# Moving the layer norm's affine by two slots in a two-layer scan kernel, with the counts that a planner reads

## The chip, the cores and the metric

The kernel runs on one core of a Trainium2 chip. The time is the device time of one execution in microseconds (us); the median of several executions is compared. A profiled execution shows what each engine did: PE (TensorE, matrix products), DVE (VectorE), ACT (ScalarE), POOL (GpSimd), and SP, whose queue issues nearly all transfers.

## What is computed

The input has 2 batches of 256 channels by 4096 positions, all in float32. Layer 0 is a state-space block (a "mamba" block); layer 1 normalises its result, runs a forward and a backward state-space block over it, and ends with a mixture of eight experts, all of which are computed for every position. Cut to what matters:

```python
# layer 0
x = x + mamba(group_norm(x))                     # inner width 256
# layer 1
t = tokens(x)
n = layer_norm(t)
xn = layer_norm(n) * ln_gamma + ln_beta          # the second norm ends with the affine
t = t + mamba_fwd(xn) + flip(mamba_bwd(flip(xn))) + n    # inner width 512
# experts, over the norm of t
f = layer_norm(t)
w = softmax(mean_over_batch(f) @ Wr + br)
t = t + sum_e w[e] * (relu(bn2(relu(bn1(f @ W1[e])) @ W2[e])) @ Wo[e] + bo[e])

def mamba(x):
    xs, z = split(x @ W_in)
    xs = silu(causal_conv4(xs))
    dt, B, C = ...                               # projections of xs, dt through softplus
    h[t] = exp(dt[t] * A) * h[t-1] + dt[t] * xs[t] * B[t]    # 16 states for each channel
    y = sum_over_states(h * C) + xs * D
    return (y * silu(z)) @ W_out
```

## The kernel before

**Tiling and order.** There are six scan jobs: for each batch, layer 0 (2 tiles of 128 inner channels), the forward block of layer 1 (4 tiles) and the backward block (4 tiles). Each job runs over 8 chunks of 512 positions. A chunk of layer 0 has 16 slots and a chunk of layer 1 has 32, so there are 1280 slots in all. Two slots make a quad: four groups of 512 positions by 128 partitions, of which each partition is one channel and state. In each slot DVE runs one scan instruction (L690) of 1024 elements, and all other work is hung on slots. `s0` is the first slot of a chunk; a slot before `s0` belongs to the chunk that runs before it.

**What a quad needs.** POOL multiplies `dt*x` by B into `bq` (L654, one operation for the quad). ACT makes the decays: it corrects the first element of a half with the carried state (the join, L675) and then takes two exponentials into a PSUM tile `da` (L664), of which there are two buffers (pool `ps_d`); it does so one slot ahead of the scan. DVE scans. The product with C is taken by DVE (L699) or, for quads 0, 2 and 5 of each 8 and some halves, by POOL (L714 copies the state out, L715 multiplies). PE then sums over the states (L723). ACT copies the state out for the halves that DVE multiplied (the carry, L709).

**What sets the order.** Each engine's instructions run in the order in which the loop over slots emits them. Within a slot the order is: SP's own work, loads that have become due, PE, PE's expert products, ACT, DVE, POOL. On ACT the carry and the decays of the next slot stand first, and what was put on the slot's "act" list follows. So late work on ACT delays the decays of the slot after the next.

**Work around the affine.** For layer 1's forward job, `norm` prepares the next chunk: `mean`, `centre`, `square`, `variance`, `roots`, `divide`, `add`, `affine` and `store` are put on slots counted from that chunk's `s0`. `affine` (L387) is two ACT operations that write `nx`, the input of the projections; `add` (L383) on POOL reads `nx` before that; `store` writes `nx` and the sum `x` to DRAM (L393, L394). In the same slots the chunk that is running ends: ACT loads the table of functions for the gate (L569) at slot 26 of its 32, the four gates' tanh (L539) run in slots 27, 28, 30 and 31, and at slot 29 ACT makes the values for the next chunk's joins (the cut, L616 and L619).

**Expert pairs.** A pair is one batch, one chunk and one expert, with three layers of two products each; each product is one entry in the plan (called an expert layer in what follows, so six to a pair), 4 PE instructions, and one ACT operation (L923, or L921 for the third layer). The pairs of the chunks whose norm is ready (`features`, in the backward jobs) are placed beside the scans by the planner in `experts`. It knows what each slot has of PE and ACT work from `sl.count(slot, products, acts, banks)`, which books PE's products on the slot and ACT's operations on the next one, and keeps two backlogs:

```python
PE_ROOM, PE_BEHIND = 3.8, 2.5
ACT_ROOM, ACT_BEHIND = 2.6, 1.2
...
                behind = max(0.0, behind) + sl.products.get(slot, 0) + sums_in(slot) - PE_ROOM
                act_behind = max(0.0, act_behind) + sl.acts.get(slot + 1, 0) - ACT_ROOM
...
                    if behind + 2 > PE_BEHIND or act_behind + 1.3 > ACT_BEHIND or not fits(slot):
                        break
```

`fits` asks whether one of three PSUM banks of the pool `psp` is free. Their results go to DRAM (`u`).

**The tail.** What is left is done after the scans: for each chunk of `rest` the pairs that are missing (L1208 for two layers, L1227 for the third), with the router's weights (`routes`: `n` loads, `nm` on POOL at L1115, logits on PE at L1122) and the sums with the results from DRAM (`sums`, L1178 and L1179) beside them. `whole` has the chunks of which all 16 pairs are done. `rest` is sorted by how many pairs of a chunk are done, and otherwise keeps the order from chunk 7 down to 0:

```python
        rest.sort(key=lambda i: sum(first[b, i] for b in range(NB)))
```

Of the kernel before, what the change touches and what calls it, by code (L numbers as in the profile page):

```python
# [131 lines left out]
def hybrid_kernel(ctx: ExitStack, tc: tile.TileContext, a: dict, out: bass.AP):  # L132
# [45 lines left out]
    def rsqrt(dst, src, eps, scale=1.0):  # L178
        nc.scalar.activation(dst, src, AF.Ln, bias=eps, scale=scale)
        nc.scalar.activation(dst, dst, AF.Exp, scale=-0.5)  # L180

    def over_channels(t):
        return t.rearrange("p (o t) -> p o t", o=1).to_broadcast([P, KC, T])


    with ExitStack() as st:
# [30 lines left out]
        sl = Slots()  # L217
# [98 lines left out]
        def norm(i):  # L316

            (job, c), ck, tag, s0 = steps[i], cks[i], tags[i], starts[i]
            s = job.cols(c)
            b = job.batch  # L320

            def alloc():
                ck["nx"] = wk.tile([P, KC, T], F32, tag="nx", name=f"nx_{tag}", bufs=2)

            if job.flip:
                def load():
                    alloc()
                    nc.sync.dma_start(ck["nx"], n2_dram[b][:, NCH - 1 - c, :, :])
                sl.put(s0 - 44, "sp", load)
                return  # L330

            def load_x():
                ck["x"] = wk.tile([P, KC, T], F32, tag="x", name=f"x_{tag}")
                src = t_dram[b] if job.layer else a["x"][b].rearrange("(k p) l -> p k l", p=P)
                nc.sync.dma_start(ck["x"], src[:, :, s])

            if job.layer == 0:
                def scale():
                    alloc()
                    for k in range(KC):  # L340
                        nc.scalar.activation(
                            ck["nx"][:, k, :], ck["x"][:, k, :], AF.Identity,
                            bias=job.gb[:, k : k + 1], scale=job.gs[:, k : k + 1],
                        )
                sl.put(s0 - 32, "sp", load_x)
                sl.put(s0 - 25, "act", scale)
                return

            def mean():
                ck["ps"] = psp.tile([P, T], F32, tag="ps", name=f"mean_{tag}")
                for k in range(KC):
                    nc.tensor.matmul(
                        ck["ps"], mean_w, ck["x"][:, k, :], start=(k == 0), stop=(k == KC - 1)
                    )

            def centre():
                ck["cen"] = wk.tile([P, KC, T], F32, tag="cen", name=f"cen_{tag}")
                nc.vector.tensor_tensor(ck["cen"], ck["x"], over_channels(ck["ps"]), ALU.subtract)  # L360

            def square():
                alloc()
                nc.scalar.activation(ck["nx"], ck["cen"], AF.Square)

            def variance():
                ck["var"] = psp.tile([P, T], F32, tag="ps", name=f"var_{tag}")
                for k in range(KC):
                    nc.tensor.matmul(
                        ck["var"], mean_w, ck["nx"][:, k, :], start=(k == 0), stop=(k == KC - 1)  # L370
                    )

            def roots():
                ck["r1"] = psp.tile([P, T], F32, tag="ps", name=f"r1_{tag}")
                rsqrt(ck["r1"], ck["var"], eps5)
                rsqrt(ck["var"], ck["var"], eps10, scale=1.0 + 1e-5)

            def divide():
                nc.vector.tensor_tensor(ck["nx"], ck["cen"], over_channels(ck["r1"]), ALU.mult)
                nc.vector.tensor_tensor(ck["cen"], ck["cen"], over_channels(ck["var"]), ALU.mult)  # L380

            def add():
                nc.gpsimd.tensor_tensor(ck["x"], ck["x"], ck["nx"], ALU.add)  # L383

            def affine():
                for k in range(KC):
                    nc.scalar.activation(  # L387
                        ck["nx"][:, k, :], ck["cen"][:, k, :], AF.Identity,
                        bias=lngb[:, 1, k : k + 1], scale=lngb[:, 0, k : k + 1],
                    )  # L390

            def store():
                nc.sync.dma_start(n2_dram[b][:, c, :, :], ck["nx"])  # L393
                nc.sync.dma_start(t_dram[b][:, :, s], ck["x"])  # L394

            for d, queue, fn in (
                (-48, "sp", load_x), (-44, "pe", mean), (-43, "dve", centre), (-42, "act", square),
                (-41, "pe", variance), (-40, "act", roots), (-39, "dve", divide), (-39, "pool", add),
                (-37 if c else -38, "act", affine), (-36, "sp", store),
            ):  # L400

                sl.put(s0 + d + (6 if c == 0 else 0), queue, fn)
            s0 += 6 if c == 0 else 0
            sl.count(s0 - 44, 2, 0, (1,))
            sl.count(s0 - 43, 0, 1)
            sl.count(s0 - 41, 2, 4, (2,))
            sl.count(s0 - 40, 0, 0, (1,))
            sl.count(s0 - 38, 0, 2)

        def in_proj(job, ck, half, j, name):  # L410
            ps = psp.tile([P, T], F32, tag="ps", name=name)
# [564 lines left out]
        for i in range(len(steps)):  # L976
            norm(i)
            prepare(i)
            load_later(i)
            finish(i)  # L980
# [420 lines left out]
```

## Time and profile before

| | us |
|---|---|
| runs, median of 3 (lowest, highest) | 5132.12 (5131.54, 5132.48) |
| the profiled execution | 5134.52 |
| its span, first to last instruction | 5132.7 |
| first scan of the second forward job (the fifth job) | at 2749.3 |
| first scan of the last backward job | at 3628.3 |
| end of the last scan | 4504.8 |
| first L1208 of the tail | 4543.7 |

| group of the profile | count | mean |
|---|---|---|
| POOL L654, `bq` from `rxdt` and B | 640 | 4543 ns |
| DVE L690, scan | 1280 | 2278 to 2350 ns (medians of its four forms) |
| ACT L664, one decay exponential | 2560 | 686 ns |
| ACT L387, half of an affine | 32 | 802 ns (median) |
| ACT L569, load of a function table | 96 | 1283 ns |
| PE L912, expert product beside the scans | 1920 | 613 to 620 ns |

Each engine is counted busy from the start to the end of its instructions. A wait is put down to what ended it. Below, "a stretch" is a span of time in us from the first instruction, and for each engine its busy time in the stretch and the number of its instructions are given.

### The profile page before, as it was taken

To read this page: it belongs to the slowest core of one execution; us is meant where nothing else is said; L and a number is where in the kernel's file an instruction comes from. 1 tells how busy PE (TensorE), PEld (TensorE's weight loads), DVE (VectorE), ACT (ScalarE), POOL (GpSimd) and SP (SyncE) were. 2 spreads that over 40 slices of the span, in tenths; PEclk is the share of its full clock that TensorE was granted. 3 is DMA by queue.
4 is the path that set the end of the run, shared out by engine and by line. 5 is a ranking of instruction groups with operands and counts; after the bars stand their busy time and mean duration, and the time that the engine had idled before them with its cause. 6 is when DMAs were issued, how large, how long until landed. Compare 5 with 4: busy or idle time off the path is not lost.

```text
span 5132.7 us, 47350 instructions
## 1 busy us (share of the span) xinstructions
PE 4283.0 (83%) x14920; PEld 1485.7 (29%) x14920; DVE 4581.7 (89%) x3088; ACT 3681.3 (72%) x7474; POOL 4410.3 (86%) x1442
## 2 busy tenths in 40 slices
PE   5677767776668988888988888899999999888999
PEld 1222222221122323333322233233333333333444
DVE  6998999999999999999989999999999999936543
ACT  5777677777767888888888788888778878832232
POOL 5998999999999999999989999999999999911100
PEclk8888888887888999999999999999999999999999
DMA  5454433344444454546654555455554444455532
GB/s 178 149 176 158 164 136 128 132 146 144 151 139 156 170 195 163 184 165 209 207 185 170 174 181 179 159 167 177 195 187 166 167 165 161 168 180 182 191 108 77
DMA packets 321355, 845.49 MB, mean 165 GB/s; under 512 B 35720, under 2 KB 107152, under 8 KB 279120
## 3 DMA queue, kind: packets, MB, share of 16 engines
q1 hardware_dynamic: 316816, 815.07, 46.2%
q0 software_dynamic: 4288, 27.40, 1.4%
q8 instruction: 118, 1.93, 0.2%
q14 instruction: 133, 1.09, 0.1%
HBM read 655.05 MB, written 187.30 MB: 164 GB/s over the span
## 4 chain that ended last, share of the span: by engine, by line
DVE 20%; PE 15%; ACT 10%; issue 4%; POOL 3%; DMA 2%; SPq 0%; DVEq 0%; POOLq 0%; ACTq 0%
DVE da L690 9%; PE hp L1208 5%; DVE bq L699 5%; ACT da L664 4%; PE y L1227 2%; PE e L912 2%; DVE bq L690 2%; POOL bq L654 2%; PE conv L452 1%; POOL bq L715 1%; PE y L723 1%; ACT bq L675 1%; DVE x L1179 1%; DVE u L1178 1%; ACT eh L923 1%
## 5 line engine op out<-in xcount | busy, mean ns | idle before, releaser
L654 POOL TENSOR_TENSOR bq<-rxdt,bc 128x2048 f32<-128x2048 f32 x640 | 2893.2, 4543 | 28.7 <-issue 12.3
L664 ACT ACTIVATE da<-rdt,w_a 128x512 f32<-128x512 f32 x2560 | 1756.8, 686 | 105.4 <-DVE bq L690 59.8
L690 DVE TENSOR_TENSOR_SCAN da<-da,h_state,bq 128x1024 f32<-128x1024 f32 x664 | 1559.1, 2348 | 50.5 <-ACT da L664 34.4
L715 POOL TENSOR_TENSOR bq<-bq,bc 128x2048 f32<-128x2048 f32 (+1 forms) x280 | 1179.9, 4214 | 22.5
L690 DVE TENSOR_TENSOR_SCAN bq<-da,h_state,bq 128x1024 f32<-128x1024 f32 x456 | 1059.3, 2338 | 28.5 <-ACT da L664 28.4
L723 PE MATMUL y<-bq,stack 128*32 128x512 f32 x5120 | 759.4, 687 | 317.4 <-POOL bq L715 297.3
L699 DVE TENSOR_TENSOR bq<-da,bc 128x1024 f32<-128x1024 f32 x760 | 926.5, 1219 | 16.0
L912 PE MATMUL e<-eh,ew 128*128 128x512 f32 x1280 | 626.1, 620 | 66.0 <-DVE sp L513 15.0
L709 ACT COPY h_state<-da 128x2 f32<-128x2 f32 x759 | 119.1, 157 | 641.3 <-DVE bq L699 639.4
L675 ACT ACTIVATE bq<-h_state,bq,a 128x1 f32<-128x1 f32 x1120 | 430.5, 384 | 0.6
L723 PEld LDWEIGHTS y<-bq,stack 128*32 128x32 f32 x5120 | 143.6, 119 | 876.7 <-POOL bq L715 404.9
L1212 ACT ACTIVATE h<-hp,of,sc 128x512 f32<-128x512 f32 x192 | 149.1, 777 | 298.9 <-PE hp L1208 281.7
L912 PEld LDWEIGHTS e<-eh,ew 128*128 128x128 f32 x1280 | 230.3, 193 | 452.0 <-issue 219.4
L414 PE MATMUL xs<-nx,w_in 128*128 128x512 f32 x640 | 318.7, 628 | 40.9 <-DVE xc L466 20.8
L452 PE MATMUL conv<-xs,w_conv 64*64 64x512 f32 x2560 | 332.6, 613 | 21.9 <-ACT xs L436 18.9
L414 PE MATMUL z<-nx,w_in 128*128 128x512 f32 x640 | 323.8, 639 | 18.7 <-DVE sp L513 10.6
L912 PE MATMUL e<-en,ew 128*128 128x512 f32 x640 | 308.3, 613 | 23.9 <-DVE fcen L809 7.8
L761 PE MATMUL o<-sz,w_out 128*128 128x512 f32 x640 | 301.7, 612 | 0.0
L923 ACT ACTIVATE eh<-e,of,sc 128x512 f32<-128x512 f32 x320 | 242.1, 768 | 36.7 <-PE e L912 36.2
L517 POOL TENSOR_TENSOR xdt<-sp,xc 128x512 f32<-128x512 f32 x160 | 203.2, 1273 | 49.9 <-DVE sp L513 49.8
L730 PE MATMUL y<-xc,w_d 128*128 128x512 f32 x320 | 193.1, 688 | 54.2 <-DVE sz L742 53.9
L690 DVE TENSOR_TENSOR_SCAN da<-da,bq 128x1024 f32<-128x1024 f32 x96 | 219.4, 2286 | 6.5 <-ACT da L664 3.6
(139 smaller groups left out, 4940.5 us busy)
## 6 DMA issues: line engine op xcount, KB each, us to landing
rxdt<-xdtd SPq DMA_DIRECT2D x160, 1024.0 KB, 6.8
rdt<-dtd SPq DMA_DIRECT2D x160, 1024.0 KB, 6.5
bc<-bcd SPq DMA_DIRECT2D x384, 256.0 KB, 3.2
dtd<-sp SPq DMA_DIRECT2D x160, 256.0 KB, 3.5
xdtd<-xdt SPq DMA_DIRECT2D x160, 256.0 KB, 4.0
ew<-in_W SPq DMA_DIRECT2D x160, 256.0 KB, 4.3
u<-u SPq DMA_DIRECT2D x80, 512.0 KB, 4.4
u<-eu SPq DMA_DIRECT2D x76, 512.0 KB, 4.0
```

Source lines behind the costliest of these rows:

```text
L414: nc.tensor.matmul(ps, job.w["in", half][:, k, j * P : (j + 1) * P], rhs, start=(k == 0), stop=(k == KC - 1),)
L452: nc.tensor.matmul(v[r][64 * col : 64 * col + 64, :], job.w["conv"][rows, 2 * jp + j, k, :], ck["xs", jp][rows, j, k : k + T] if k < 4 els ...
L654: nc.gpsimd.tensor_tensor(bq[g], ck["rxdt", j], over_groups(ck["bc", 0, sg]), ALU.mult)
L664: nc.scalar.activation(da[g, h][:, k, :], cks[i]["rdt", j][:, q, :], AF.Exp, scale=steps[i][0].w["a"][:, j, q * SG + sg : q * SG + sg + 1],)
L675: nc.scalar.activation(bq[g][:, q, 0:1], job.h[:, j, sg, q : q + 1], AF.Identity, scale=cks[i]["a0", j][:, h, sg : sg + 1], bias=bq[g][:, ...
L690: nc.vector.tensor_tensor_scan(b if on_pool(g, h) else d, d, b, job.h[:, j, sg, 2 * h : 2 * h + 1] if c else 0.0, ALU.mult, ALU.add,)
L699: nc.vector.tensor_tensor(bq[g][:, two, :], d, cks[i]["bc", 1, sg].rearrange("p (o t) -> p o t", o=1).to_broadcast([P, 2, T]), ALU.mult,)
L715: nc.gpsimd.tensor_tensor(b, b, cks[i]["bc", 1, sg].rearrange("p (o t) -> p o t", o=1).to_broadcast([P, groups, T]), ALU.mult,)
L723: nc.tensor.matmul(y[i, j][q * CG : (q + 1) * CG, :], stack, bq[g][:, q, :], start=False, stop=(sg == SG - 1),)
L761: nc.tensor.matmul(v[m], job.w["out"][:, j, m * P : (m + 1) * P], ck["sz", j], start=False, stop=(j == job.nj - 1),)
L912: nc.tensor.matmul(ps, ew[l][:, k, m * P : (m + 1) * P], key[x][:, k, :], start=(k == 0), stop=(k == KC - 1),)
L923: nc.scalar.activation(key[dst][:, m, :], key["ps", l, m], AF.Relu, bias=of[:, l, e, m : m + 1], scale=sc[:, l, e, m : m + 1],)
```

## The change

`affine` of chunks 1 to 7 is put two slots later (from slot `s0 - 37` to `s0 - 35`); that of chunk 0 keeps its slot. `store` of all chunks is put two slots later. What the planner is told of the affine changes: for chunks 1 to 7 it is booked on ACT two slots later, for chunk 0 one slot earlier, where it runs, and with 2.3 operations instead of 2.

```diff
@@ norm
                 (-41, "pe", variance), (-40, "act", roots), (-39, "dve", divide), (-39, "pool", add),
-                (-37 if c else -38, "act", affine), (-36, "sp", store),
+                (-35 if c else -38, "act", affine), (-34, "sp", store),
             ):
 
                 sl.put(s0 + d + (6 if c == 0 else 0), queue, fn)
...
             sl.count(s0 - 40, 0, 0, (1,))
-            sl.count(s0 - 38, 0, 2)
+            sl.count(s0 - (36 if c else 39), 0, 2.3)
```

Nothing else is edited. The planner places the pairs anew from these counts, so the slots of expert work, the number of pairs beside the scans, and `first`, `rest` and the order of chunks in the tail follow from them.

## The prediction

> **What bounds the kernel now.** I read the page first (parts 1 and 2), then busy time by stretch, then the waits of POOL and of DVE in the same stretches, then single places on the timeline. From the page:
>
> ```profile
> span 5132.7 us, 47350 instructions
> PE   5677767776668988888988888899999999888999
> DVE  6998999999999999999989999999999999936543
> ACT  5777677777767888888888788888778878832232
> POOL 5998999999999999999989999999999999911100
> ```
>
> Up to the 35th slice (4505 us) DVE and POOL are both full; then PE alone is. So there are two regimes: the scans, and a tail of 628 us with the expert pairs that were not done beside the scans. The stretches are the first forward scan of layer 1 (526.70), the second (2749.30), chunks 1 to 6 of the second backward scan (3737.50), and the tail's pairs (4543.70):
>
> ```profile
> core 0: us, PE busy (x) PEld busy (x) DVE busy (x) ACT busy (x) POOL busy (x), PEclk, DMA share, GB/s
> 526.70:1399.20 872.50, 609.89 (x2310) 182.02 (x2312) 855.16 (x557) 635.76 (x1341) 867.99 (x278) 0.82 0.40 140
> 2749.30:3628.30 879.00, 779.17 (x2851) 267.89 (x2850) 856.62 (x557) 715.89 (x1476) 870.43 (x278) 0.95 0.51 174
> 3737.50:4399.70 662.20, 596.57 (x2182) 206.05 (x2181) 641.70 (x415) 533.11 (x1115) 646.45 (x205) 0.96 0.51 173
> 4543.70:5113.40 569.70, 546.06 (x1321) 238.76 (x1322) 277.82 (x262) 168.63 (x228) 75.44 (x54) 0.97 0.43 153
> ```
>
> In the scans POOL has only 4.5, 8.6 and 15.8 us free, DVE 17.3, 22.4 and 20.5. A microsecond of DVE idle costs time only where POOL comes to wait for it. POOL's waits are listed in one row of each stretch that the change touches (the first forward scan has no such row at all); the first row is the second forward scan, the others the second backward scan without its last chunk, POOL then DVE:
>
> ```profile
> POOL h_state L714 <- DVE bq L690: 4.0, 4, 1.5
> ...
> POOL h_state L714 <- DVE bq L690: 12.4, 10, 1.5
> ...
> DVE bq L690 <- ACT da L664: 11.1, 7, 2.2
> DVE da L690 <- ACT da L664: 6.4, 9, 1.8
> ```
>
> Now the place that the change is about: the affine (L387) and the first gate (thz) of chunk 2 to 3 of the second forward scan, on ACT, then the DVE scan that came late by it, then POOL at that moment:
>
> ```profile
> 3063.66 0.58 ACT L539 ACTIVATE thz<-z 128x512 f32<-128x512 f32 x1
> 3064.14 1.51 ACT L387 ACTIVATE nx<-cen,lngb 128x512 f32<-128x512 f32 x2
> 3065.55 0.37 ACT L675 ACTIVATE bq<-h_state,bq,a 128x1 f32<-128x1 f32 x1
> ...
> 3063.81 2.36 DVE L690 TENSOR_TENSOR_SCAN da<-da,h_state,bq 128x1024 f32<-128x1024 f32 x1 [0.45 <-issue]
> ...
> 3062.87 2.35 POOL L715 TENSOR_TENSOR bq<-bq,bc 128x1024 f32<-128x1024 f32 x1
> 3065.17 4.55 POOL L654 TENSOR_TENSOR bq<-rxdt,bc 128x2048 f32<-128x2048 f32 x1
> ```
>
> DVE lost 0.45 us; POOL ran on without a gap, so this stall was paid for already. And a stall of another kind, in the second backward scan:
>
> ```profile
> 3973.66 1.42 ACT L664 ACTIVATE da<-rdt,w_a 128x512 f32<-128x512 f32 x2 [1.79 <-DVE bq L690]
> ...
> 3971.28 2.34 DVE L690 TENSOR_TENSOR_SCAN bq<-da,h_state,bq 128x1024 f32<-128x1024 f32 x1
> 3975.11 2.35 DVE L690 TENSOR_TENSOR_SCAN bq<-da,h_state,bq 128x1024 f32<-128x1024 f32 x1 [1.48 <-ACT da L664]
> ```
>
> Here the decay exponentials of a scan could start only when the scan just before it had ended: they were given the PSUM buffer of that scan instead of the other of the two. DVE stood for 1.48 us.
>
> [...] the gap of 1.48 us comes again at the same slot of chunks 0, 1, 2, 3, 5 and 6 of the backward scan. [...] In this trace they nearly agree (L654 lasts 4.55 us, and two in a row start 4.50 us apart), so I use POOL's waits as they stand.
>
> **The change part by part.**
>
> Affine two slots later (14 of 16 chunks; chunk 0 keeps its slot). It adds no instruction. It takes 1.51 us of ACT from a slot that lasts 2.26 us and puts it into one of 3.97 us. There it meets the cut (L616, L619: 0.47 + 0.30), often one expert activation (0.77) and the standing work (carry 0.17, join 0.40, decays 1.42): 5.04 us of ACT, 1.07 more than the slot. The next slot is 3.52 us with about 3.3 us of ACT work; together 8.4 against 7.5, but the decays must be in time, not the trailing expert work (1.35 us), so I charge nothing. The affine overwrites what POOL's add reads; its waits for that (3.0 us in 4 cases) can only shrink. The consumer, the input projection, is still four slots away. First forward scan: POOL never waits, gain 0. Second: at most the 4.0 us of POOL's waits.
>
> Stores two slots later. The two stores of a chunk (n2 and t) move on SP's queue past one rxdt load (chunk 0: past one weight load), in the second scan past an expert weight load too; these are now issued ahead of them. Behind the stores stand bc1 loads (3.2 us from issue to landing in part 6), first wanted some four slots (13 us) later. Cost 0; if that cover went, at most 3 us a chunk. The x buffer, read by the store, is wanted again some 18 slots later: 0.
>
> The planner's counts. This is the larger effect. Evaluating the planning loop with the new counts gives 81 pairs instead of 80 (on PE the built order has 486 rows of expert matmuls for 480). Expert layers per chunk of the second forward scan go from 16 14 16 17 15 16 21 20 to 16 16 18 18 18 18 22 19; both versions leave 8 layers after the last scan. Three consequences:
>
> 1. One pair fewer in the tail. PE is busy 546.1 of 569.7 us there, so it is the bound; a pair is 24 matmuls, and undisturbed pairs follow each other every 10.6 us (L1208 at 5063.8, 5074.4, 5085.0). Gain 10.6. The pair taken over is batch 1, chunk 5, expert 0, which moves chunk 5 from first to last of the tail; with chunk numbers renamed the rest of the sequence is the same, its largest wait (PE for POOL's nm, 12.4 us) included: 0. Its addition costs two DVE operations and one load of 512 KB, beside PE: 0.
>
> 2. The extra pair beside the scans: 14 us of PE and 4.3 us of ACT, spread over slots with ACT free for some 20 us a chunk: 0, apart from stalls in item 3.
>
> 3. Another pattern of expert work per slot. In the order of the built kernels with their waits, the decays of the sixth slot of a 16-slot group wait for DVE (the bad buffer) in 21 groups of 80 before and in 15 after; the six that go are chunk 4 of the second forward scan and chunks 1, 2, 3, 5, 6 of the second backward scan. No new one appears. Each is 1.48 us of DVE: 7.4 in the backward scan. In exchange five chunks there take the pattern that chunks 3 and 6 of the forward scan had, which shows 0.6 us of idle DVE at slots 6 and 7, but loses the 0.64 at slot 18. What comes back is bounded by POOL's 12.4 us of waits. DVE needs 107 us busy plus about 2 idle, POOL about 108, per chunk of 110.4: I take 8. Bounds: 3 (the new pattern eats most) to 12.4. In the forward scan, of POOL's 4.0: chunk 4's wait (1.0) goes with its stall, of chunk 7's 2.6 about half, since its bad buffer stays. I take 2.5, bounds 0 and 4.
>
> Last chunk of the scans: 34 layers for 36, two bad buffers stay: 0 ± 1.5. Passage to the tail (38.9 us): the same 8 layers and stores: 0 ± 1.
>
> Sum: 10.6 + 8 + 2.5 = 21.1. The profiled execution took 5134.5 us (span 5132.7 and 1.8 around it), so 5113.4; the median of the runs, 5132.1, is 2.4 lower: 5111.
>
> **The rivals.**
> A. Only the tail gains: POOL holds the pace in the backward scan as well, or the new pattern's stalls replace the old. For it: POOL's 646 of 662 us. Against: 12.4 us of waits. 5132.1 - 10.6 = 5121.5, to 5119.
> B. Every DVE stall was time: DVE, not POOL, sets the scans. For it: DVE at 97%; the affine's stalls and chunk 6's 2.1 us at slots 27 and 28 (about 4.5), six bad buffers (8.9), chunk 0's 4.0 at slots 27 and 28 of the backward scan, a forward-scan stall of 2.2: about 20, with 10.6 some 31, so 5101. Against: POOL without gaps at the affine.
> C. Slower: the denser packing makes ACT late. For it: chunk 1 of the second forward scan, where an ACT copy waited for PE and DVE then stood 2.2 us at slot 7. If each of the twelve chunks 1 to 6 of the two later scans paid that (26), and each of seven affines the 1.07 us of its overfull slot (7.5), with POOL's slack used up, it would be 34 - 7.4 for the bad buffers - 10.6 = +16: 5148. It decides from 18 us in all, 1.4 a chunk. Against: ACT is free for 20 us of such a chunk, and chunks 3 and 6, which had the dense start, lost 0.6.
> D. The change does less than it says: the 81st pair is done beside the scans but the tail gives its 10.6 back at the reordered end, by waits of PE for the last chunk's sums. About 5122, or 5130 if the scans gain nothing too.
>
> **How the numbers follow.** Forecast 0.62, A 0.17, B 0.12, C 0.05, D 0.04. The forecast's own bounds: the least of it is 10.6 + 3 + 0 - 1.5, 5120, the most 10.6 + 12.4 + 4 + 1.5, 5103.6. A's end takes the range to 5121, the nearer part of B to 5102. A measurement of this kernel can tell about 0.2% from no change, 10.3 us, that is 5121.9. The forecast, B and 0.12 of A lie below it: 0.86; D and the other 0.05 of A: 0.09; C: 0.05.
>
> **What would show it.** The tail's pairs, from first L1208 to last, about 10.6 us shorter, and the end of the last scan about 10 us earlier. POOL's waits for DVE in the second backward scan 4 to 5 us instead of 12.4; the 1.48 us stall gone in five of six chunks. The first forward scan within 1 us of 872.5 although its affine moved. I am wrong in mechanism if the first forward scan shortens by several us, or if POOL's waits fall and the stretch does not; wrong in size if the tail's wait for nm grows beyond 12.4.

## The result and the profile after

The changed kernel takes 5111.89 us (median; 5107.34 to 5113.05), the kernel before 5131.83 us in the same series. The ratio is 0.9961 (95% interval 0.9951 to 0.9971), so 20 us or 0.4% less. The prediction was 5111. The profiled execution has a span of 5111.0 us, 21.7 below the 5132.7 of before.

First the page's head and its slices of the changed kernel, in the rows of before:

```profile
span 5111.0 us, 47355 instructions
...
PE   5777767776668988988888889999999999988999
...
DVE  6998999999999999999989999999999999936633
ACT  5777677777767888888887888888878888832232
POOL 5998999999999999999989999999999999921110
```

The two regimes are as they were; nothing new is full. Where the time went shows only by stretch. The rows give start and end, length, then busy time of PE, PE's loads, DVE, ACT and POOL, the clock, the DMA share and GB/s. They are the first forward scan, the second, chunks 1 to 6 of the second backward scan, the passage from the last scan to the first L1208, and the tail's pairs:

```profile
526.30:1398.80 872.50, 607.67 (x2310) 181.47 (x2312) 855.08 (x556) 635.57 (x1341) 867.99 (x278) 0.82 0.40 139
2748.90:3625.10 876.20, 787.06 (x2890) 271.56 (x2889) 857.08 (x556) 721.17 (x1486) 869.99 (x278) 0.96 0.52 177
3732.90:4389.90 657.00, 599.93 (x2177) 202.72 (x2176) 641.91 (x415) 533.89 (x1113) 647.30 (x206) 0.97 0.52 173
4495.00:4533.70 38.70, 25.18 (x62) 10.04 (x62) 1.95 (x3) 7.40 (x11) 2.32 (x5) 0.87 0.35 121
4533.70:5092.30 558.60, 532.14 (x1297) 232.53 (x1298) 276.62 (x263) 165.60 (x225) 74.49 (x54) 0.97 0.45 158
```

Against before: 0 in the first forward scan, 2.8 less in the second, 5.2 less in the six backward chunks (chunk 0 of that scan gave 1.4 more), 0.2 in the passage, 11.2 in the tail. The last scan ended at 4495.0 instead of 4504.8. POOL's busy time in the backward row did not fall (646.45 to 647.30) while the row fell by 5.2; so it is POOL's waiting that went. DVE's busy time did not fall either (641.70 to 641.91), so its idle time fell as much. These are POOL's waits in the second forward scan and in backward chunks 1 to 6, then DVE's in the latter (total us, times, longest):

```profile
POOL h_state L714 <- DVE bq L690: 1.5, 1, 1.5
...
POOL h_state L714 <- DVE bq L690: 6.3, 6, 1.5
...
DVE sp L513 <- ACT h_state L709: 8.4, 6, 2.1
DVE da L690 <- ACT da L664: 2.3, 6, 0.7
DVE xc L466 <- ACT thx L461: 1.4, 5, 0.3
```

POOL's waits were 4.0 and 12.4. DVE's waits in the same six chunks of the kernel before:

```profile
DVE bq L690 <- ACT da L664: 7.4, 5, 1.5
DVE sp L513 <- ACT h_state L709: 5.8, 6, 1.1
DVE da L690 <- ACT da L664: 4.2, 7, 0.7
```

Its first row, which holds the five stalls of 1.48 us, is gone. In exchange the softplus on DVE (L513) waits 8.4 us for ACT where it waited 5.8. One row fell and another grew: the experiments had to take these apart.

One reading in the prediction was wrong. It showed 0.45 us of idle DVE beside the affine as the affine's stall. This is the same place of the changed kernel, ACT first and then DVE:

```profile
3058.17 1.28 ACT L569 ACT_TABLE_LOAD   x1
3059.47 0.78 ACT L923 ACTIVATE eh<-e,of,sc 128x512 f32<-128x512 f32 x1
3060.14 0.38 ACT L675 ACTIVATE bq<-h_state,bq,a 128x1 f32<-128x1 f32 x1
3060.42 1.40 ACT L664 ACTIVATE da<-rdt,w_a 128x512 f32<-128x512 f32 x2
...
3067.70 1.51 ACT L387 ACTIVATE nx<-cen,lngb 128x512 f32<-128x512 f32 x2
...
3061.91 2.36 DVE L690 TENSOR_TENSOR_SCAN da<-da,h_state,bq 128x1024 f32<-128x1024 f32 x1 [0.45 <-POOL h_state L714]
```

The affine is now 6 us away and the gap is still 0.45 us. The scan starts when its decays end (3060.42 + 1.40), and these stood behind the table load (1.28 us) and an expert activation (0.78). Before, too, the affine started only after that scan had (3064.14 against 3063.81), so it cannot have held it up; the lines shown in the prediction already said so. Neither place shows a scan that came late by the affine.

### The profile page after: what moved, and what is told of

It is laid out like the page before. It is cut to its first block, busy times and chain, and to the rows that moved or that the text cites. A ratio compares the mean times of both kernels' runs of the same rounds, so it can differ in the third digit from the quotient of the medians.

```text
span 5111.0 us, 47355 instructions
## 1 busy us (share of the span) xinstructions
PE 4272.0 (84%) x14920; PEld 1474.5 (29%) x14920; DVE 4580.6 (90%) x3089; ACT 3682.0 (72%) x7476; POOL 4409.1 (86%) x1442
## 5 line engine op out<-in xcount | busy, mean ns | idle before, releaser
L709 ACT COPY h_state<-da 128x2 f32<-128x2 f32 x759 | 118.9, 157 | 617.7 <-DVE bq L699 615.4
L452 PE MATMUL conv<-xs,w_conv 64*64 64x512 f32 x2560 | 332.1, 608 | 21.7 <-ACT xs L436 17.8
```

Source lines behind the costliest of these rows:

```text
L452: nc.tensor.matmul(v[r][64 * col : 64 * col + 64, :], job.w["conv"][rows, 2 * jp + j, k, :], ck["xs", jp][rows, j, k : k + T] if k < 4 els ...
```

## The experiments

All runs beside the kernel before on the same chip. The last table of this section has their stretches.

**1. The affine alone.** The planner's counts as before, so the old plan with 80 pairs:

```diff
-                (-37 if c else -38, "act", affine), (-36, "sp", store),
+                (-35 if c else -38, "act", affine), (-34, "sp", store),
```

> The kernel before with the affine and the stores two slots later, but with the old planner counts, so 80 pairs and the old pattern of expert work. My theory: POOL has no gap at the affine, so moving it gives nothing: 5132 us, within 2 us of before; the 32 reused PSUM buffers and POOL's 12.4 us of waits in the second backward scan stay. Rival (the affine's place matters): half or all of the gain outside the tail, 5 to 9 us, so 5123 to 5127, with the forward scans shorter.

Measured: ratio 0.9999 (0.9991 to 1.0007), median 5131.96 us. The move that gave the change its name is worth nothing that can be measured; a rival that needed 5 us or more lies outside the interval. In its profile the second forward scan was 2.1 us shorter (876.9), POOL's waits there 2.0 instead of 4.0, which the total does not resolve.

**2. The counts alone.** The affine and the stores at their old slots:

```diff
-            sl.count(s0 - 38, 0, 2)
+            sl.count(s0 - (36 if c else 39), 0, 2.3)
```

> The kernel before with only the new planner counts: affine and stores at their old slots, 81 pairs, the new pattern of expert work. My theory: nearly all of the gain, 5112 us within 2, with the backward scan shorter by some 6.6 us as in the changed kernel. Rival (the affine has to make room first): ACT is too full at the old slots, 5115 to 5121.

Measured: ratio 0.9960 (0.9948 to 0.9972), median 5112.49 us. This one line is the whole gain. Chunks 1 to 6 of the backward scan took 657.8 us, as in the changed kernel; the affine does not have to make room. The line makes three changes at once, which were not timed one by one. Worked out with the planning loop alone, the 2.3 by itself leaves the old plan as it is, and the shift of chunks 1 to 7 by two slots gives the new 81 pairs, with one expert layer one slot off; with the booking of chunk 0 moved too it is the new plan exactly.

**3. The changed kernel without the 81st pair.**

```diff
-            emit_experts(put)
+            emit_experts(put[:80])
```

> The changed kernel with everything of its plan but the 81st pair (batch 1, chunk 5, expert 0), which goes back to the tail. My theory: the tail's pairs cost 10.6 to 11.2 us each, so 5122.5 to 5123 us, with the end of the last scan where the changed kernel has it (4495, at most 1 us earlier). Rival D of the prediction (the tail gives the pair back by its order): 5112 to 5114.

Measured: ratio 0.9967 (0.9954 to 0.9980), median 5115.83 us, where I had expected 5122.5 to 5123. The median is 4 us above that of the changed kernel, but the two intervals overlap, and the profiled execution, the fastest of its executions, is no longer than the changed kernel's (span 5110.2 against 5111.0). So the pair is worth between nothing and some 4 us, and not 11. These are the passage and the tail of this kernel:

```profile
4494.20:4522.00 27.80, 14.55 (x39) 5.57 (x37) 1.90 (x2) 3.12 (x5) 1.93 (x4) 0.83 0.39 131
4522.00:5091.10 569.10, 546.53 (x1321) 238.59 (x1322) 277.57 (x262) 168.84 (x228) 75.39 (x54) 0.97 0.44 154
```

The tail got its pair back (569.1, 10.5 more), but the passage became 10.9 shorter. In the chain of waits of the changed kernel and then of this one, one sees why (start, length, what):

```profile
4521.11 2.89 DMA u<-eu
4524.00 0.02 SPq L1201
...
4525.96 8.02 DMA W<-in_W
```

```profile
4508.77 0.59 ACT xr L776
4509.36 0.02 issue
4509.38 3.06 DMA t_dram<-xr
...
4515.35 6.62 DMA bo<-in_bo
4521.97 0.01 issue
4521.98 6.70 PE hp L1208 x10
```

In these two chains the loads for the tail follow the landing of the last store of the part before: with the 81st pair that is the pair's result `u`, at 4524.0; without it, the last output of the scan itself, at 4512.4. The plan shows that all six layers of the 81st pair come after the last scan, where eight layers are left both before and after the change. So the pair that the change adds is worth little as a pair. What shortens the whole is that six more layers were done before the last scan ended: 478 in the changed kernel and in this one, 472 before. Passage and tail together took 608.7 us before, 597.2 in the changed kernel, and 596.9 here, with the 80 pairs of before. My expectation forgot the passage; it does not speak for rival D, since the tail's own length did return.

**4. The kernel before, without reused buffers.**

```diff
-            da[g, h] = ps_d.tile([P, 2, T], F32, tag="da", name=f"da_{g}_{h}")
+            da[g, h] = ps_d.tile([P, 2, T], F32, tag=f"da{h}", name=f"da_{g}_{h}", bufs=1)
```

The PSUM used and the order of all instructions are the same; only which of the two buffers a decay gets differs, in that the two halves of a quad now always have different ones.

> The kernel before with the decays' two PSUM buffers given out by turns, one for the first and one for the second scan of each group; all instructions and their order stay, and no decay gets the buffer of the scan just before it any more (32 did). My theory: the gain of the changed kernel in the second backward scan came from six such buffers, so here the same stretch of six chunks goes from 662 to about 656 us, and all 32 together give 1.1 us where POOL was waiting too, about 18 us (8 to 25): 5114 us. Rival B (each stall of DVE is time): 32 times 1.48, 47 us: 5085. Rival (the pattern of expert work, not the buffers, made the backward scan shorter): 5130 to 5132.

Measured: ratio 0.9956 (0.9944 to 0.9968), median 5110.34 us, as much as the whole change, from a line that the change does not touch. The row of chunks 1 to 6 of the second backward scan, and POOL's waits in it:

```profile
3724.20:4377.70 653.50, 590.55 (x2183) 208.08 (x2182) 640.95 (x416) 533.12 (x1115) 647.03 (x205) 0.97 0.52 175
```

```profile
POOL h_state L714 <- DVE bq L690: 3.1, 4, 1.4
...
DVE sp L513 <- ACT h_state L709: 5.6, 6, 1.1
```

8.7 us less than before, for five stalls of 1.48 (7.4 us) that fell into them; chunk 4, which had no such stall, changed by 0.2 (109.4 to 109.2). So the buffers did cost this time, and in this place in full; the 1.3 us beyond the stalls are not explained. The last scan ends 25.6 us earlier than before; layer 0 of batch 1 alone gave 8.3 (465.0 to 456.7) for 11 buffers. The 47 us of rival B were set too high, because not every reused buffer stops DVE for 1.48 us: in layer 0 the trace shows such a stall as 0.90 us, and some of the 32 show none. DVE's idle time just before these 32 scans was 35.1 us in the kernel before and is 9.1 here: 26.0 less, of which 25.6 came back by the end of the last scan. So for these stalls rival B's assumption, that a stall of DVE is time, nearly holds in the sum. Job by job it is rougher: 3.6 us less idle time for 1.1 us in the first layer-0 job, 5.8 for 8.3 in the second. My 18 us, taken from POOL's waits, were somewhat low; the medians are 22 apart.

**5. The changed kernel without reused buffers**: the same line, on the changed kernel.

> The changed kernel with the decays' two PSUM buffers given out by turns, so that the 26 reused ones go; instructions and order stay. The kernel before gained 22 us by the same edit, of which some 9 in the two scans in which the change already gained. My theory: the two gains overlap only there, so 5112 less 13 to 16: 5096 to 5099, and with no reused buffer left the pattern of expert work gives nothing more: chunks 1 to 6 of the second backward scan within 1.5 us of the 653.4 that the kernel before had with such buffers. Rival (the new pattern is a gain of its own): 5112 less 22, 5090, and these chunks below 651. Rival (the new pattern costs, and only hid that behind the buffers): above 656.

Measured: ratio 0.9931 (0.9919 to 0.9944), median 5097.51 us. The total is as expected, the stretch is not. The row of backward chunks 1 to 6, then the waits in it:

```profile
3723.90:4381.20 657.30, 599.39 (x2178) 202.56 (x2177) 642.13 (x416) 534.50 (x1113) 647.70 (x206) 0.97 0.52 173
```

```profile
POOL h_state L714 <- DVE bq L690: 6.2, 6, 1.5
...
DVE sp L513 <- ACT h_state L709: 7.6, 5, 2.6
...
DVE sp L513 <- POOL bq L715: 0.9, 1, 0.9
```

657.3 and not 653.4: for the stretch the third theory was right. With no reused buffer on either side, the new pattern of expert work is 3.8 us slower than the old, 2.9 of it in chunk 1 (111.5 against 108.6 us). The changed kernel, which has no reused buffer in these chunks either, took 657.0. In the change the two effects are thus -8.7 for the buffers and about +3.7 for the pattern.

One place of that cost, in chunk 1: ACT in the kernel before, then ACT and DVE in the changed one:

```profile
3816.16 0.60 ACT L508 ACTIVATE sp<-dt 128x512 f32<-128x512 f32 x1 [2.03 <-DMA dtd<-sp]
```

```profile
3811.87 0.60 ACT L508 ACTIVATE sp<-dt 128x512 f32<-128x512 f32 x1 [3.31 <-DMA dtd<-sp]
...
3813.97 0.69 DVE L513 SCALAR_TENSOR_TENSOR sp<-dt,sp 128x512 f32<-128x512 f32 x1 [2.09 <-ACT h_state L709]
```

In both kernels ACT started this softplus when an earlier one had been stored (`dtd<-sp`) from the same buffer; that store took 5.7 us from issue to release (3806.16 to 3811.87) instead of 4.4 (3811.73 to 3816.16). The carry (L709) that DVE waited for came after the softplus on ACT, at 3813.79 and, before, at 3818.08; DVE's wait grew from 0.81 to 2.09. The buffer is one of three of the tag `th`, shared with the gates and the norm's squares. The wait goes with the plan: at this place ACT waits 2.0 and 2.1 us in the kernel before and in run 4, 3.3 and 3.8 in the changed kernel and in run 5. Over the six chunks DVE waits 5.6 us before the softplus in run 4 and 8.5 here (the two rows shown), which is 2.9 of the 3.8. A fourth buffer was not tried, so it is not shown that this wait is the cause, and why the store takes longer under the new plan is open. DVE's stalls at slots 6 and 7 (0.6 us in each of chunks 2 to 5 and 1.3 in chunk 1) belong to the new pattern too.

**6. The affine done twice**, which leaves the result as it is: some 20 us more of ACT (1.4 us in each of 14 chunks), in slots that the prediction had counted as overfull.

```diff
-                for k in range(KC):
+                for k in [*range(KC)] * (2 if c else 1):
```

> The changed kernel in which the affine of every chunk but the first of a forward scan is done twice, the second over the first with the same values: 1.51 us more of ACT in a slot that was already fuller than it lasts, in 14 chunks, 21 us of ACT in all. The planner's counts stay. My theory: ACT has 20 us free per chunk and POOL sets the pace, so what DVE loses is paid already: 5112, at most 3 more. Rival C of the prediction (an overfull slot of ACT is paid in time): 14 times 1.5, 5133; in the first forward scan alone 872.5 would become 883.

Measured: ratio 0.9963 (0.9950 to 0.9977), median 5112.98 us. The two forward scans:

```profile
528.10:1400.60 872.50, 609.45 (x2310) 183.52 (x2312) 855.17 (x556) 643.33 (x1353) 868.00 (x278) 0.82 0.40 140
2750.90:3627.00 876.10, 785.15 (x2890) 269.57 (x2889) 857.68 (x557) 729.04 (x1498) 869.88 (x278) 0.96 0.53 178
```

ACT is busy some 8 us longer in each (six of the chunks fall into each row), and the stretches are as long as in the changed kernel. DVE does not wait longer either: in the first forward scan its waits come to 13.7 us in the changed kernel and to 13.6 here. So the longer affine did not even reach DVE, and whether POOL's pace would have covered a stall of DVE was not put to the test. Rival C is out as far as it rested on the affine's slot.

**7 and 8. More pairs beside the scans**, on the kernel of run 5, since there is still room on PE. Run 7 lets the planner be further behind, run 8 books more room:

```diff
-PE_ROOM, PE_BEHIND = 3.8, 2.5
+PE_ROOM, PE_BEHIND = 3.8, 3.0
```

```diff
-PE_ROOM, PE_BEHIND = 3.8, 2.5
+PE_ROOM, PE_BEHIND = 4.0, 2.5
```

> As the changed kernel with buffers by turns, but the planner lets PE be behind by 3.0 instead of 2.5, which gives 88 pairs beside the scans instead of 81, and 12 expert layers after the last scan instead of 8. My theory: PE has some 13 us free per chunk and seven more pairs ask 3 to 4 of them, so the tail gets shorter by 7 times 10.6, 74 us, and the passage longer by 4 layers, 7 us: 5098 - 67 = 5031. Rival C in a new form (the denser packing makes PE and ACT late in the scans): each of some 30 chunks pays 1.4 to 3 us, 42 to 90 us: 5073 to 5120.

> As the changed kernel with buffers by turns, but the planner counts 4.0 instead of 3.8 of PE's time as room in a slot: 89 pairs beside the scans instead of 81, 12 layers after the last scan. My theory: eight pairs less in the tail, 85 us, 7 us more in the passage: 5098 - 78 = 5020. Rival C in a new form: the scans pay 42 to 90 us, 5062 to 5110.

Measured: 5083.98 us, ratio 0.9907 (0.9893 to 0.9920), and 5085.54 us with the same ratio and interval. Both beat all kernels above. The first theory was wrong by 53 and 66 us. Both totals lie in the range of rival C's new form, but not for its reasons alone: in run 7, against run 5, the scans end 26 us later, where it had 42 to 90, the passage is 9 longer, and seven pairs shortened the tail by only 50 us, 7.2 each, where both theories had taken 10.6. The tail's row and PE's waits:

```profile
4557.80:5065.70 507.90, 461.87 (x1129) 203.19 (x1130) 288.63 (x269) 144.07 (x196) 76.59 (x54) 0.94 0.51 180
```

```profile
PE lt L1122 <- POOL nm L1115: 25.2, 2, 14.0
PE var_m L1108 <- ACT sq L1105: 13.7, 1, 13.7
```

PE is busy 462 of 508 us there, and waits 25.2 and 13.7 us in rows that had 16.7 and 2.4 in the changed kernel: with fewer pairs to cover them, the tail's other chains begin to show. So the price of 10.6 us a pair holds near 80 pairs and not at 88. And the scans do pay for denser packing: the second forward scan takes 888.2 us in run 7, against 875.4 in run 5, and POOL's waits in it are 9.0 against 0.7.

**9. Run 7 without its last two pairs**, `put[:86]`.

> As the run with 88 pairs, without its last two pairs, whose layers fall after the last scan (10 of the 12 that are left there); they go back to the tail. In the run with the 81st pair dropped the passage to the tail became 11 us shorter and the tail 11 us longer. My theory: a pair whose layers come after the last scan is worth nothing, since the tail waits for its output to be stored: the passage goes from 47 to about 28 us, the tail gets 14 to 21 us longer, so 5079 to 5086. Rival (each pair done early is worth its tail price): 5098 to 5105.

Measured: 5093.29 us, ratio 0.9925 (0.9911 to 0.9938); neither theory. The passage went from 47.2 to 29.1 us, as the first theory had it. But from the first L1208 to the end it took 25.8 us more (527.0 to 552.8), where two pairs at 10.6 are 21. PE's busy time there grew by 23.3 us (475.6 to 498.9) and its idle time only from 51.4 to 53.9. The waits moved: a new one stands at the tail's end,

```profile
PE y L1227 <- DVE h L1219: 24.5, 2, 16.8
```

while those for `nm` and for the square (L1105) fell from 25.2 and 13.7 us to 15.8 and 2.4. So two pairs that end after the last scan were worth 7 to 9 us here (the spans are 6.7 apart, the medians 9.3), neither nothing nor their full price, and which pairs are left decides where the tail waits.

The stretches of all profiled executions in us (the scans from one chunk's first scan to the next one's; the tail from the first to the last L1208):

| kernel | 1st forward | 2nd forward | 2nd backward, chunks 1-6 | end of last scan | passage | tail | span |
|---|---|---|---|---|---|---|---|
| before | 872.5 | 879.0 | 662.2 | 4504.8 | 38.9 | 569.8 | 5132.7 |
| changed | 872.5 | 876.2 | 657.0 | 4495.0 | 38.7 | 558.5 | 5111.0 |
| 1 affine only | 872.6 | 876.9 | 662.8 | 4503.9 | 37.3 | 568.9 | 5129.3 |
| 2 counts only | 872.5 | 876.6 | 657.8 | 4494.0 | 38.0 | 560.0 | 5110.7 |
| 3 pair dropped | 872.6 | 876.7 | 656.7 | 4494.2 | 27.8 | 569.1 | 5110.2 |
| 4 buffers, before | 871.4 | 876.2 | 653.5 | 4479.2 | 37.6 | 571.4 | 5107.5 |
| 5 buffers, changed | 871.4 | 875.4 | 657.3 | 4484.4 | 37.8 | 558.2 | 5099.1 |
| 6 affine twice | 872.5 | 876.0 | 657.1 | 4498.6 | 38.1 | 557.3 | 5112.7 |
| 7 88 pairs | 871.3 | 888.2 | 662.3 | 4510.6 | 47.2 | 507.9 | 5084.8 |
| 8 89 pairs | 871.4 | 879.3 | 663.6 | 4519.1 | 48.0 | 499.8 | 5085.7 |
| 9 86 pairs | 871.4 | 887.9 | 662.7 | 4509.7 | 29.1 | 504.2 | 5091.5 |

The backward column carries the main argument. All five kernels with the plan of the change lie at 656.7 to 657.8, whether or not the affine was moved; with the old plan it is 662.2 and 662.8, and 653.5 without reused buffers. The stretch less POOL's waits is nearly one number: 662.2 - 12.4 = 649.8 before, 657.0 - 6.3 = 650.7 changed, 653.5 - 3.1 = 650.4 in run 4, 657.3 - 6.2 = 651.1 in run 5. But so is the stretch less DVE's waits: 662.2 - 17.4 = 644.8, 657.0 - 12.1 = 644.9, 653.5 - 9.7 = 643.8, 657.3 - 12.2 = 645.1. Both engines do nearly the same work in all four, so these sums do not tell which of the two sets the pace. For POOL speaks the first forward scan, where DVE waits 13.6 us and POOL has no row of waits; in run 4, on the other hand, DVE's idle time came back nearly in full (25.6 of 26.0 us). That idle time of DVE costs only where POOL comes to wait for it was my assumption, and is not shown.

## Why the prediction was right, point by point

- **Affine, 0 in the first forward scan**: right (872.5 in both), and shown by runs 1, 2 and 6. The reason given, that ACT's lateness was paid already because POOL had no gap, is not shown: the stall named for it was not the affine's, and even the doubled affine of run 6 did not make DVE wait longer (13.6 us, 13.7 in the changed kernel).
- **Stores two slots later, 0**: nothing speaks against it; run 1 has them moved and is equal. They were not tried alone.
- **Tail, 10.6**: measured 11.2, right in size. The working was right that eight layers are left after the last scan in both kernels; that this condition carries the 10.6 was seen only in run 3.
- **The extra pair beside the scans, 0 apart from item 3**: not quite, since its pattern cost about 3.7 us in the backward scan. This is the term that was mis-sized: "I take 8, bounds 3 to 12.4" became 5.2 in chunks 1 to 6, and 6.6 with chunk 0. Its two halves were both off: the buffers gave 8.7 where 7.4 stood, and the new pattern, judged by the idle time at slots 6, 7 and 18 alone, took back more. Those slots did cancel as it said in chunks 2, 3 and 5 (0.6 us against 0.6); most of the rest is idle time of DVE at slot 23, where ACT waits for a store (DVE's waits at L513: 8.4 us instead of 5.8). POOL's waits fell to 6.3 and not to 4 to 5.
- **Six reused buffers gone**: right. The stall is gone in chunks 1, 2, 3, 5 and 6 of the backward scan and in chunk 4 of the second forward scan. It came not from too few buffers, but from which of two was given: run 4 has as many and gains 22 us.
- **Second forward scan, 2.5**: measured 2.8, but not for the reason given alone. Runs 1, 2 and 4, each with a different edit, all shortened it by 2 to 3 us; 4.0 us of POOL's waits is all there was to gain, and which edit got how much is open.
- **Not in the sum**: the backward scan of batch 0 was 2.6 us shorter and layer 0 of batch 1 2.5 longer. They cancel; their cause was not looked into. That the total came within 1 us is therefore partly luck: the backward scan gave 1.4 less than its 8, the tail 0.6 and the second forward scan 0.3 more, and these two terms, which nobody had counted, took each other away.

Rivals: A is out by the backward column. B is out by its total, since 5101 lies below the interval of the ratio (5107 to 5117 us); its assumption is not refuted, and nearly holds for the buffers of run 4. C is out by the total, and by run 6 for the affine; its other half, dense packing, appears in run 7. D is out by the tail, which is 11.2 us shorter.

## What to carry to other kernels

A label in a planner can matter more than the instruction that it stands for, as it did here (ratio 0.9960 for the counts alone, 0.9999 for the affine alone): try the moved instruction and the moved count one at a time. With two engines both nearly full (DVE 97% and POOL 98% of backward chunks 1 to 6), the waits of one gave the price of the other's stalls only roughly here, 18 us for a measured 22: take the stall out and time it, as run 4 did. Price a task taken out of the tail by what is left when the tail starts: the 81st pair, taken out of the tail but still holding up its first loads, gained nothing to 4 us where 10.6 stood. Where a gap repeats at one slot behind a pool of two buffers, look at which buffer is given before asking for more: run 4 took 22 us out with the same two.

## What was not expected of the hardware

A store of 256 KB, issued at about the same point of a chunk in two plans (74.2 and 73.3 us after its first scan), took 4.4 us until its buffer was free in the kernel before and 5.7 us in the changed one; 1.3 us in a transfer that nobody had counted showed in full as idle time of DVE (0.81 to 2.09). And in run 6, 8 us more of ACT work (643.3 us instead of 635.6) in the first forward scan moved its length of 872.5 us by nothing at all.
